# A relational graph convolution on one core: below tile 420, half as many tiles fetched by single row copies

## The chip, the cores and the metric

The kernel runs on one core of one Trainium2 chip. The metric is the device time of one execution in microseconds, the median of several runs. A profile comes from one further execution. Its engines are called PE (TensorE), DVE (VectorE), ACT (ScalarE), POOL (GpSimd) and SP (SyncE); "PEld" is PE's loading of weights.

## What is computed

There are 12500 nodes with 256 features each and 212500 edges, sorted by their destination; every node has one edge to itself. Each edge has one of eight types.

```
h   = relu(layernorm(x))                       # 12500 x 256
hx  = einsum('ni,rio->rno', h, weight)         # one product for each of 8 types
msg = hx[edge_type, src]                       # one row for each edge
agg = segment_sum(msg, dst)                    # 12500 x 256
out = x + agg * sqrt(0.5) + bias + (h @ loop_weight) * sqrt(0.5)
```

## The kernel before, in words

The kernel first sums and then multiplies: for each node and type it adds up the rows of h of the edges that end there, and only then multiplies with the type's weights. So the work has two halves.

**Edge tiles.** The edges are cut into tiles of 128. There are 1581 of them, two to a unit, in the order of the destinations. For tile t, the 128 rows of h of its edges' sources are brought from HBM into a buffer `msg[t]` of SBUF, 128 partitions by 256 numbers, 131 KB. DVE makes a one-hot matrix (line 967) that says for each edge to which of some 13 or 17 near destinations and which type it belongs. PE multiplies the two (line 1005, `edge_sums`; four matmuls a tile in the profile), and DVE adds a unit's sums to a ring of accumulators in SBUF (line 1031).

**Groups of nodes.** When the last edge of a group of 128 nodes is in, PE multiplies the group's sums with the weights (line 1187, `product`), DVE adds x (lines 1200, 1201), and SP writes four groups at a time to the output (line 1206).

**How the rows come.** The first 100 tiles or so are gathered from x and normalised in SBUF, while h is being made and written to HBM; all later ones come from h. There are two ways to bring a tile.

- *Gathered*: one instruction on GpSimd's queue (`gather`, line 915), an indirect DMA with 128 row numbers.
- *Fetched row by row*: 128 copies of one row of 1 KB each (`load_sources` and `fetch_row`, line 939). The SP queue issues rows 0 to 31 and 64 to 95, the ACT queue the other 64. The row number is loaded into a register first. The copies count up one of four semaphores, and PE waits for that count before the tile's sums (`edge_sums`).

`single_rows(t)` decides which tiles are fetched: one in 28 (`SINGLE`), t mod 28 = 27, once h has been ready for long enough, and not in the last 16 tiles. The first such tile is 167 and the last 1539; these are 50 tiles, 6400 row copies. The other 1531 tiles are gathered.

**What sets the order.** The program is written out by hand as a loop over t with fixed places for all work; each engine's queue runs in that order. In step t the loop issues gathers up to tile `goal(t)`, which stands 64 tiles ahead of t until t = 170, then less by one every five tiles, down to 24 from t = 370 on. A gather waits for the sums of the unit that was the last in the program when it was issued ("no faster than the sums"). The buffers `msg` hold 66 tiles (33 pairs). A fetched tile is begun (`begin_fetch`) 36 tiles ahead of its sums (`FAR`), or further ahead where the gathers stand further ahead; its loads come 8 steps later (`HOLD`), and then the loop issues up to four row copies on each of the two queues in each step (`FETCH`). A fetch also waits until the sums of the fetched tile four before it are done, as there are four counters.

The same SP queue issues the 512 KB loads of x and h for the groups (line 1137), the writes of the output (line 1206) and the loads of the indices (line 393); ACT's queue issues small loads of indices (line 405). ACT also clears some of the ring at the beginning (line 1040).

Of the kernel before, what the change touches and what calls it, by code (L numbers as in the profile page):

```python
# [62 lines left out]
SINGLE = 28  # L63
# [2 lines left out]
BY_SP = (0, 2)  # L66
HOLD = 8
FAR = 36
COUNTERS = 4


# [173 lines left out]
def kernel(  # L245
# [64 lines left out]
    def place_of(t):  # L310
        u, i = divmod(t, PAIR)
        half = 0 if PAIR * u + 1 == NT else PAIR - 1 - i
        b, row = row_of(u)
        return b, half, row


    with ExitStack() as main:
# [32 lines left out]
        single, fetches = {}, {SP: [], ACT: []}  # L350
        counters = [tc.alloc_semaphore(f"rows{i}") for i in range(COUNTERS)]
        fetched, summed = {}, {}
# [532 lines left out]
        def single_rows(t):  # L885

            return (t % SINGLE == SINGLE - 1 and t + 2 * NEAR < NT
                    and state["h32"] is not None and t // QUAD * QUAD >= state["h32"] + LATE + AHEAD)

        def begin_fetch(t):  # L890

            if t not in msg:
                room(t - t % PAIR)
            fetched[t] = len(fetched)
            for k, r in enumerate(range(0, P, SOURCES)):
                engine = SP if k in BY_SP else ACT
                fetches[engine].append((
                    done["tile"] + HOLD,
                    lambda r=r, engine=engine: load_sources(t, r, engine)))

        def gather(t):
            if t % PAIR == 0 and t not in msg:
                room(t)
            if t % QUAD:
                kind[t] = kind[t - 1]
            else:
                kind[t] = "h" if state["h32"] is not None and t >= state["h32"] + LATE else "x"
            table = {"h": h32, "x": x}[kind[t]]
            b, i, u = place_of(t)
            if single_rows(t) and t not in fetched and t - done["tile"] >= FAR:  # L910
                begin_fetch(t)
            if t in fetched:
                return
            at = i * P + u
            i = nc.gpsimd.indirect_dma_start(  # L915
                out=msg[t], out_offset=None, in_=table[:, :],
                in_offset=bass.IndirectOffsetOnAxis(ap=gidx[b][:, at : at + 1], axis=0))
            if "unit" in latest:
                tc.add_manual_dep(
                    i.ins, latest["unit"], SYNC_DEP, reason="no faster than the sums")  # L920

        def goal(t):

            lead = max(NEXT, AHEAD - max(0, t - NARROW) // SLOPE)
            lead = min(lead, max(CLOSE, (NT - t) // SLOPE))
            return min(t + lead + 1, STARTED + STEEP * (t // PAIR * PAIR))

        def load_sources(t, r0, engine):
# [9 lines left out]
            def fetch_row(i, v):  # L938
                j = queue.dma_start(
                    msg[t][r0 + i : r0 + i + 1, :].bitcast(U8), h32_bytes[:, bass.ds(v, D * 4)])  # L940
                j.then_inc(counters[k % COUNTERS], 16)
                tc.no_tile_sem_insts.add(j.ins.name)
                tc.add_to_no_dep_group(f"rows{t}", j.ins)
                if i == 0 and k >= COUNTERS:
                    tc.add_manual_dep(
                        j.ins, summed[k - COUNTERS], SYNC_DEP, reason="counter is at rest")

# [37 lines left out]
        def edge_sums(t):  # L985
# [14 lines left out]
            if t in fetched:  # L1000
                k = fetched[t]
                j = nc.tensor.wait_ge(counters[k % COUNTERS], 16 * P * (k // COUNTERS + 1))
                tc.declare_fence(j.ins, group=f"rows{t}")
# [229 lines left out]
        with tc.manual_schedule():  # L1233
# [129 lines left out]
            for t in range(NT):  # L1363
                done["tile"] = t
                if t + FAR >= gathered and single_rows(t + FAR):
                    begin_fetch(t + FAR)
                while gathered < min(NT, goal(t)):
# [125 lines left out]
```

## Time and profile before

| | |
|---|---|
| time, median of 3 runs (lowest to highest) | 1981.88 us (1979.95 to 1982.96) |
| the profiled execution's own time | 1982.09 us |
| span of its profile, first to last instruction | 1980.4 us |
| mean granted clock of PE | 0.949 |
| row copies on the SP queue, on the ACT queue | 3200, 3200 |
| gathers from h, from x | 1431, 100 |
| DMA over the span | 279.45 MB, mean 141 GB/s |

Busy time in the page is the time in which an engine worked on something; "idle before" stands with the group in front of which the engine had nothing to do, and the name behind the arrow is what ended that. A DMA that GpSimd issues counts as busy time of GpSimd for as long as it is being issued, not until the data is there. Issues on the SP and ACT queues aren't counted as busy at all; they are seen in the timeline and in the view of a line.

### The profile page before, as it was taken

What the parts mean: (1) busy time and instruction counts of PE and PEld (TensorE: products, weight loads), DVE (VectorE), ACT (ScalarE), POOL (GpSimd) and SP (SyncE); (2) the same over time, 40 slices, a digit from 0 to 9 for tenths busy, and PEclk for the clock granted to TensorE, in tenths of its full rate; (3) what the DMA queues carried; (4) which work ended last, traced back from release to release, by engine and by line L of the source; (5) the groups of instructions that cost most, each with busy time, mean ns of one, the idle gap of its engine ahead of it and who ended that gap; (6) DMA issues with size and microseconds to landing.
All of it is one profiled execution on the core that took longest, in us unless ns stands there. A gap on an engine that the chain in (4) does not pass through costs nothing. (4 is left out here: it accounts for less than half of the span.)

```text
span 1980.4 us, 41340 instructions
## 1 busy us (share of the span) xinstructions
PE 1711.7 (86%) x10161; PEld 1473.8 (74%) x10161; DVE 1309.2 (66%) x3272; ACT 159.2 (8%) x334; POOL 1457.9 (74%) x1557
## 2 busy tenths in 40 slices
PE   2348999998899888889998898888989989899998
PEld 1247898997777777778777777777777767687897
DVE  6769767886665677656678565578666567665653
ACT  6777200000000000000000000000000000000000
POOL 7677776677777777777777777777777777777774
PEclk8559999999999999999999999999999999999999
DMA  7993444443444444444434444444444344444432
GB/s 252 358 301 103 126 126 134 140 140 107 138 128 122 149 132 120 141 130 121 149 111 141 132 119 143 141 119 141 129 122 142 109 144 130 120 140 125 127 115 78
DMA packets 158363, 279.45 MB, mean 141 GB/s; under 512 B 35376, under 2 KB 109126, under 8 KB 158118
## 3 DMA queue, kind: packets, MB, share of 16 engines
q0 software_dynamic: 73488, 200.77, 34.5%
q1 hardware_dynamic: 76584, 72.73, 11.9%
q10 hardware_dynamic: 8046, 3.30, 0.9%
q8 instruction: 80, 1.31, 0.3%
q14 instruction: 165, 1.35, 0.2%
HBM read 251.06 MB, written 25.60 MB: 140 GB/s over the span
## 5 line engine op out<-in xcount | busy, mean ns | idle before, releaser
L915 POOL DMA_INDIRECT msg<-h,gidx x1431 | 1361.2, 951 | 458.6 <-issue 335.6
L1005 PEld LDWEIGHTS ps<-oh,msg 128*128 128x128 f32 x6324 | 942.1, 198 | 408.1 <-DMA msg<-h,gidx 258.7
L1005 PE MATMUL ps<-oh,msg 128*128 128x136 f32 (+2 forms) x6324 | 1022.8, 291 | 226.3 <-DMA msg<-h,gidx 139.0
L1187 PE MATMUL po<-w,acc 128*128 128x256 f32 x3136 | 891.0, 389 | 15.4 <-DVE acc L1031 15.3
L1031 DVE TENSOR_TENSOR acc<-acc,ps 128x352 f32 x791 | 408.8, 517 | 413.0 <-PE ps L1005 402.1
L1187 PEld LDWEIGHTS po<-w,acc 128*128 128x128 f32 x3136 | 519.0, 193 | 52.1 <-DVE acc L1031 18.6
L1069 DVE SCALAR_TENSOR_TENSOR acc<-types,pt 128x256 f32<-128x256 bf16 (+1 forms) x688 | 247.3, 411 | 67.6 <-PE pt L1051 61.9
L967 DVE TENSOR_TENSOR oh<-fixed,cols 128x544 f32<-128x544 f32 (+1 forms) x396 | 285.8, 722 | 0.0
L915 POOL DMA_INDIRECT msg<-in_x_dram,gidx x100 | 94.8, 948 | 41.4 <-issue 30.1
L1187 PE MATMUL po<-wl,self_t 128*128 128x256 f32 x392 | 115.5, 420 | 3.5 <-DVE acc L1031 1.8
L1187 PEld LDWEIGHTS po<-wl,self_t 128*128 128x128 f32 x392 | 73.8, 210 | 12.6 <-DVE acc L1031 3.1
L853 ACT ACTIVATE msg<-msg,shift,rstd 128x256 f32<-128x256 f32 x100 | 50.8, 586 | 4.4 <-DVE stats L817 3.6
L853 ACT ACTIVATE xt<-xt,shift,rstd 128x256 f32<-128x256 f32 x98 | 50.0, 587 | 7.0 <-DVE shift L850 6.1
L809 DVE BATCH_NORM_STATS2 stats<-xt 128x6 f32<-128x256 f32 x98 | 34.3, 412 | 23.5 <-DMA xt<-in_x_dram 22.7
L1200 DVE TENSOR_TENSOR xr<-xr,po 128x256 f32<-128x256 f32 x98 | 40.4, 412 | 13.4 <-PE po L1187 12.2
L1123 DVE CAST types<-pt 128x512 bf16<-128x512 f32 x22 | 15.2, 691 | 49.6 <-PE pt L1119 49.6
L1056 DVE COPY self_t<-pt 128x256 f32<-128x256 f32 x98 | 40.7, 415 | 8.5 <-PE pt L1051 5.4
L1051 PE MATMUL pt<-ident,hr 128*128 128x128 f32 x196 | 38.9, 281 | 7.2 <-DMA hr<-h 5.3
L442 DVE TENSOR_SCALAR moves<-fixed 128x271 int32<-128x271 int32 (+1 forms) x90 | 40.6, 452 | 4.4 <-DVE acc L1031 3.0
L1201 DVE TENSOR_TENSOR xr<-xr,po 128x256 f32<-128x256 f32 x98 | 41.2, 421 | 3.4
L444 DVE COPY_PREDICATED fixed<-moves,fixed 128x311 int32<-128x311 int32 (+14 forms) x90 | 38.0, 422 | 3.1
L1051 PEld LDWEIGHTS pt<-ident,hr 128*128 128x128 f32 x196 | 25.6, 153 | 10.6 <-DMA hr<-h 5.6
(162 smaller groups left out, 349.1 us busy)
## 6 DMA issues: line engine op xcount, KB each, us to landing
msg<-h ACTq DMA_DIRECT2D x3200, 1.0 KB
msg<-h SPq DMA_DIRECT2D x3200, 1.0 KB
msg<-h,gidx POOLq DMA_INDIRECT x1431
xt<-in_x_dram SPq DMA_DIRECT2D x24, 512.0 KB
h<-xt SPq DMA_DIRECT2D x24, 512.0 KB
xr<-in_x_dram SPq DMA_DIRECT2D x24, 512.0 KB
hr<-h SPq DMA_DIRECT2D x24, 512.0 KB
out_dram<-xr SPq DMA_DIRECT2D x24, 512.0 KB
```

Of the source, the lines that this page charges most:

```text
L442: nc.vector.tensor_single_scalar(m, packed[:, :n], 1 << (bit + k), op=ALU.bitwise_and)
L853: nc.scalar.activation(row, row, AF.Relu, bias=shift[:n, j : j + 1], scale=rstd[:n, j : j + 1])
L915: i = nc.gpsimd.indirect_dma_start(out=msg[t], out_offset=None, in_=table[:, :], in_offset=bass.IndirectOffsetOnAxis(ap=gidx[b][:, at : at ...
L967: j = nc.vector.tensor_tensor(o[:, k : k + v, :i, :width], iota_f[:, :width].unsqueeze(1).unsqueeze(1).to_broadcast([P, v, i, width]), of. ...
L1005: j = nc.tensor.matmul(ps[:, c, first : first + width], m[:, c * P : (c + 1) * P], o[:, :width], start=(i == 0 and c == 0), stop=(end and ...
L1031: i = nc.vector.tensor_tensor(a, a, ps, op=ALU.add)
L1051: in_run("turns", nc.tensor.transpose(pst[:, c, :n], rows_[:n, c * P : (c + 1) * P], ident[:n, :n]), c == KC - 1)
L1056: nc.vector.tensor_copy(got["self", g][:, :, :n], pst[:, :, :n])
L1069: i = nc.vector.scalar_tensor_tensor(acc[:, :, r, s0 : s0 + n], of, float(r + 1), pst[:, :, :n], op0=ALU.is_equal, op1=ALU.mult)
L1187: i = nc.tensor.matmul(got["out", g][:n], lhs, rhs, start=(r == R and c == 0), stop=(r == R - 1 and c == KC - 1))
L1200: nc.vector.tensor_add(rows_[:n, k, :], rows_[:n, k, :], outs[g % 2][:n, 1, :])
L1201: nc.vector.tensor_add(rows_[:n, k, :], rows_[:n, k, :], got["out", g][:n])
```

## The change

`single_rows` gets one more condition. From tile 420 (`SPARSE`) on it decides as before. Below 420 only tiles with t mod 56 = 27 are still fetched row by row; the others are issued by `gather` as any other tile, in their place in GpSimd's queue.

```diff
+SPARSE = 420
@@ def single_rows(t):
             return (t % SINGLE == SINGLE - 1 and t + 2 * NEAR < NT
+                    and (t >= SPARSE or t % (2 * SINGLE) == SINGLE - 1)
                     and state["h32"] is not None and t // QUAD * QUAD >= state["h32"] + LATE + AHEAD)
```

The function is asked in the loop (for tile t + 36) and in `gather`. Nothing else in the text of the kernel changes. The counters of the fetched tiles are given out in turn, so later fetches use other ones of the four than before.

## The prediction

> **What bounds the kernel now.** I read the costliest groups of the page first, then the chain that ended last, then GpSimd's line by stretches of time. The question was which engine's lateness becomes the end.
>
> ```profile
> PE 1711.7 (86%) x10161; PEld 1473.8 (74%) x10161; DVE 1309.2 (66%) x3272; ACT 159.2 (8%) x334; POOL 1457.9 (74%) x1557
> ...
> L915 POOL DMA_INDIRECT msg<-h,gidx x1431 | 1361.2, 951 | 458.6 <-issue 335.6
> L1005 PEld LDWEIGHTS ps<-oh,msg 128*128 128x128 f32 x6324 | 942.1, 198 | 408.1 <-DMA msg<-h,gidx 258.7
> ...
> L915 POOL DMA_INDIRECT msg<-in_x_dram,gidx x100 | 94.8, 948 | 41.4 <-issue 30.1
> ```
>
> GpSimd is 74% busy by the first row, yet its gathers and the idle time in front of them are 1361.2 + 458.6 + 94.8 + 41.4 = 1956.0 us of the 1980.4 us span. PE's weight loads wait 258.7 us for gathers. In a quiet place, GpSimd alone (the timeline: start, duration, instruction, idle time before it):
>
> ```profile
> 700.09 0.95 POOL L915 DMA_INDIRECT msg<-h,gidx  x1 [0.30 <-PE ps L1005]
> ...
> 711.34 0.95 POOL L915 DMA_INDIRECT msg<-h,gidx  x1 [0.30 <-issue]
> ```
>
> Ten gathers, nine steps, 11.25 us: a gather costs **1.25 us** of GpSimd, 0.95 busy and 0.30 that is there before every one of them. The end hangs on the last gather (the chain that ended last, in order of time):
>
> ```profile
> 1953.92 0.95 POOL msg L915
> 1954.86 0.30 issue
> 1955.17 2.79 DMA msg<-h,gidx
> 1957.96 0.04 issue
> 1958.00 0.86 PE ps L1005 x4
> ```
>
> So the last 26 us begin with one of GpSimd's last gathers and its landing, and what follows is PE's. A gather more costs 1.25 us, and a pause of GpSimd beyond 0.30 us costs its length, unless GpSimd is held back anyway.
>
> Where does it pause? First two stretches from the groups view limited to a window (count; busy, mean ns; idle before): 230 to 286 us and 286 to 566 us.
>
> ```profile
> L915 POOL DMA_INDIRECT msg<-h,gidx x45 | 42.6, 948 | 14.1 <-issue 10.4 <-PE ps L1005 2.5 <-DMA msg<-h,gidx 0.9
> ```
>
> ```profile
> L915 POOL DMA_INDIRECT msg<-h,gidx x210 | 199.3, 949 | 80.9 <-issue 44.3 <-DMA msg<-h,gidx 21.1 <-PE ps L1005 14.0
> ```
>
> Then 566 to 902 us, as long as both together, from the view of line 915 (idle time and number of times, by what ended it):
>
> ```profile
> L915 POOL DMA_INDIRECT msg<-h,gidx x267: 940/946/1279, 565.1 to 901.1; - x134
> ...
>   issue: 64.5, 207
>   PE ps L1005: 9.5, 31
>   DMA msg<-h,gidx: 6.7, 22
>   PE po L1187: 1.2, 4
> ```
>
> From 230 to 286 us the idle time is 14.1 / 45 = 0.313 us a gather. From 566 to 902 us it is about 82.8 / 267 = 0.310 (the four rows and 0.9 in smaller ones). From 286 to 566 us it is 80.9 / 210 = 0.385. **The excess is 80.9 - 210 x 0.310 = 15.8 us**; against 0.313 it is 15.2, against the bare 0.30 it is 17.9.
>
> What are the pauses? The same view says below who waited for line 915. The first fence is 230 to 566 us (its first row is still of the list of idle time), the second 566 to 902 us:
>
> ```profile
>   PE ps L1005: 16.5, 39
> ...
>   POOL msg L915: 23.9, 41
> ```
>
> ```profile
>   PEld ps L1005: 62.5, 88
>   PE ps L1005: 33.3, 49
> ```
>
> In the first stretch GpSimd's own gathers waited 41 times for an earlier gather to land; in the second only PE did. The pauses that the view puts down to PE I count with these, since the same gathers wait for both; if they are PE's own, 16.5 - 39 x 0.30 = 4.8 us of the excess would stay. One pause is of another kind: 1.95 us at 293.47, ended by nothing that the profile shows.
>
> ```profile
> 284.90 0.94 POOL L915 DMA_INDIRECT msg<-h,gidx  x1 [0.71 <-PE ps L1005]
> ...
> 288.06 0.94 POOL L915 DMA_INDIRECT msg<-h,gidx  x1 [0.97 <-DMA msg<-h,gidx]
> ...
> 293.47 0.94 POOL L915 DMA_INDIRECT msg<-h,gidx  x1 [1.95 <-issue]
> ...
> 304.57 0.95 POOL L915 DMA_INDIRECT msg<-h,gidx  x1 [1.41 <-DMA msg<-h,gidx]
> ```
>
> Why are landings late just there? The row copies of line 939 are densest there (issues on the ACT and SP queues, first 230 to 566 us, then 566 to 902 us):
>
> ```profile
> L939 ACTq DMA_DIRECT2D msg<-h x767: 217/228/825, 229.7 to 565.8; - x192
> ...
> L939 SPq DMA_DIRECT2D msg<-h x704: 227/228/1229, 232.4 to 558.6; - x176
> ```
>
> ```profile
> L939 ACTq DMA_DIRECT2D msg<-h x641: 227/228/761, 566.1 to 901.8; - x161
> ...
> L939 SPq DMA_DIRECT2D msg<-h x610: 227/228/937, 580.3 to 901.8; - x153
> ```
>
> 1471 rows in 336 us are 4.4 a us; 1251 are 3.7 a us, and there GpSimd doesn't pause. The two queues run one tile's fetch after the other (the timeline of ACT's queue):
>
> ```profile
> 229.68 23.33 ACTq L939 DMA_DIRECT2D msg<-h  x64
> ...
> 255.52 6.39 ACTq L939 DMA_DIRECT2D msg<-h  x19
> ...
> 262.04 96.90 ACTq L939 DMA_DIRECT2D msg<-h  x237
> ```
>
> A fetch of 64 rows takes 23.3 us of a queue. The first pause comes at 284.90, after two fetches on end: one fetch does not do it, a chain of them does.
>
> **The change, part by part.** Fetched row by row are the tiles with t mod 28 = 27 from 167 on; below 420 these are 167, 195, ..., 419, ten. The new condition keeps t mod 56 = 27: 195, 251, 307, 363, 419. **Out go 167, 223, 279, 335 and 391.** From 447 on nothing changes in the rule.
>
> *Added: five gathers on GpSimd.* 5 x 1.25 = **+6.25 us**. They come while GpSimd is the engine that sets the end, so nothing hides them. If each were as long as the longest above, 1279 ns in place of 946, it would be 7.9 us; less than 5 x 0.95 = 4.7 can't be.
>
> *Removed: 5 x 128 row copies, with the register loads in front of them.* On the queues this is 5 x 23.3 us each, off the path: no engine's work waits for a queue in the chain that ended last. Removed on PE: five waits on a counter of rows. PE had no idle time at all at 230 to 286 us (56.00 busy of 56.00, below), so I cost them at nothing; covered they are by PE's own queue of work.
>
> *Moved: the density of the rows.* Without the five, the stretch 230 to 566 us has 1471 - 640 = 831 rows, 2.5 a us, well below the 3.7 at which GpSimd doesn't pause. Nor can the rest bunch up: a fetch's buffer is that of a tile 66 back, so the next kept fetch can't start until PE is there, some 56 tiles after the last one's.
>
> ```profile
> 230.00:286.00 56.00, 56.00 (x375) 51.88 (x372) 33.90 (x70) 3.82 (x2) 42.02 (x45) 1.00 0.49 142
> 286.00:566.00 280.00, 264.11 (x1662) 235.14 (x1661) 201.26 (x482) 0.00 (x0) 199.25 (x210) 0.98 0.45 128
> 566.00:902.00 336.00, 301.22 (x1784) 253.12 (x1784) 217.83 (x517) 0.00 (x0) 253.51 (x267) 0.96 0.45 132
> ```
>
> Columns: PE, weight loads, DVE, ACT, GpSimd busy with counts, granted clock, DMA share, GB/s. Line 1005 has four matmuls a tile, so its count gives PE's pace:
>
> ```profile
> 230.00:566.00 336.00, 192.01 (x1268) 185.72 (x1267) 0.98 0.46 131
> 566.00:902.00 336.00, 178.36 (x1112) 161.05 (x1111) 0.96 0.45 132
> ```
>
> 317 tiles in the first 336 us, 1.06 us a tile: 56 tiles take 59 us, in which a queue fetches for 23.3 us. One fetch and then a rest is what the trace shows before its first pause. **So of the 15.8 us I let 14.0 go**: the odd 1.95 us pause (1.65 over the usual 0.30) stays, and 0.2 us for a chance meeting with a 512 KB load. The ends are 0 and 17.9.
>
> *What is late next.* PE must use the time. It is full at first (56.00 of 56.00), but that is while it has gathered tiles in stock; from 566 to 902 us it waits for gathers:
>
> ```profile
> L1005 PE MATMUL ps<-oh,msg 128*128 128x104 f32 (+1 forms) x1112 | 178.7, 288 | 34.8 <-DMA msg<-h,gidx 33.6
> ```
>
> 33.6 us of idle time in 336 us: PE takes up a lead of 8 us in about 80 us, long before the end. Then GpSimd bounds as before.
>
> **Sum**, against the profiled execution's own 1982.1 us: 1982.1 + 6.25 - 14.0 = 1974.3. The median of the runs shown, 1981.9, is 0.2 below that execution, so I forecast **1974.1 us**.
>
> The rule that bears on the disputed term: the Trainium skill, page "DMA: Bandwidth & Descriptors", section "Why a DMA increments its semaphore by 16 and not by 1", says that a copy issued from SP or ACT runs on k of the 16 engines, the lowest-numbered, with k set by the shape, while a GpSimd transfer counts all 16. By it a copy of one row could lie on few engines, or one, which every gather needs too; then the whole excess goes with the rows, as I have it. No row here names an engine.
>
> **The rivals.**
>
> *Slower: landings are late by the sum of the traffic.* A gathered tile moves the same bytes as a fetched one. If the 16 DMA engines' common load makes landings late, the pauses stay, and the five gathers are added: 1981.9 + 6.25 = 1988.1 us. It decides from the point where the DMA share, not the rows a us, goes with the pauses. For it: the pauses end with landings. Against it: the share is 0.45 with the pauses and 0.45 without (above), and 0.49 at 230 to 286 us without. Chance 0.09. The same page's section "Issuing engines are not separate DMA queues" speaks for this rival: whoever starts a DMA, it runs on the same 16 engines. The equal shares in the trace don't agree that this is all.
>
> *No change: half of the pauses stay.* One fetch of 23 us may be enough when a 512 KB load falls into it, or when the kept fetches from 363 on still meet. Then 7 us go: 1981.9 + 6.25 - 7 = 1981.1 us. For it: pauses are found up to 566 us, where PE is no longer full. Against it: 566 to 902 us has the loads and no pauses. Chance 0.16.
>
> *More than forecast.* The odd pause goes too and GpSimd runs at the bare 0.30: 1981.9 + 6.25 - 17.9 = 1970.2 us; this is the forecast's own lower end.
>
> That the change doesn't do what it says is excluded by the count of tiles above.
>
> **How the numbers follow.** Forecast 0.75 (1970.2 to 1978), half 0.16, slower 0.09. The range is 1970 to 1981: it leaves out the slower rival and the upper half of the second, 0.17. About 0.2%, 4 us, is what a measurement of this kernel can tell from no change: faster than 1977.9 us 0.75, within 0.15, slower than 1985.8 us 0.10.
>
> **What would show it.** GpSimd: 1436 gathers from h in place of 1431. From 286 to 566 us some 221 gathers in place of 210 with idle time near 0.31 us each, and hardly a wait of a gather for a gather. Row copies: 2880 on each queue, about 830 in all from 230 to 566 us. From 566 us on the same 0.31. I am wrong if the pauses are there with 2.5 rows a us (the slower rival), or if GpSimd's pauses go and PE's waits for gathers after 566 us grow instead of the end coming nearer.

## The result, and the profile after

The kernel after takes **1977.7 us** (median of 10 runs, 1974.7 to 1979.8), the kernel before 1983.0 in the same comparison (10 runs, 1980.0 to 1988.2). The ratio is **0.9968, 95% interval 0.9959 to 0.9976**, that is 5.3 us faster. The forecast was 7.8 us faster. In two series of the runs below (e1 to e4 and e7 to e9) the kernel before took 2400 us in place of 1980; the same kernels were run again where it took 1980 (e5 and e10 to e12), and those runs decide.

The profiled execution of the kernel after took 1979.8 us, the longest of the ten. Line numbers are larger by one or two than before: 917 is the gather, 941 the row copy. First the stretch of the pauses, 286 to 566 us, GpSimd's group of gathers (count; busy, mean ns; idle before):

```profile
L917 POOL DMA_INDIRECT msg<-h,gidx x224 | 213.1, 951 | 68.4 <-issue 53.4 <-PE ps L1007 7.3 <-DMA msg<-h,gidx 5.5
```

224 gathers where there were 210, and 68.4 / 224 = 0.305 us of idle time each in place of 0.385. I take 0.305 as the bare rate below; the kernel before has the same from 690 to 810 us, 29.3 / 96 (shown further down), where no gather waits longer. Who waited for line 917 in that stretch (us, times):

```profile
  PEld ps L1007: 8.6, 12
  POOL msg L917: 5.5, 18
  PE ps L1007: 4.8, 7
```

Gathers still wait for gathers 18 times, but 5.5 / 18 = 0.31 us is the usual gap: the pauses are gone. The row copies from 230 to 566 us:

```profile
L941 ACTq DMA_DIRECT2D msg<-h x452: 217/228/907, 251.8 to 566.0; - x151
...
L941 SPq DMA_DIRECT2D msg<-h x384: 227/228/367, 251.9 to 550.1; - x192
```

836 rows, 2.5 a us, as forecast. So far the profile is the one that was forecast. But here is a place that was not, GpSimd from 690 to 810 us, before and after:

```profile
L915 POOL DMA_INDIRECT msg<-h,gidx x96 | 91.3, 952 | 29.3 <-issue 21.4 <-PE ps L1005 4.9 <-DMA msg<-h,gidx 2.4
```

```profile
L917 POOL DMA_INDIRECT msg<-h,gidx x92 | 87.2, 948 | 33.6 <-issue 24.7 <-DMA msg<-h,gidx 4.3 <-PE ps L1007 3.1
```

Four gathers fewer, and 33.6 - 92 x 0.305 = **5.5 us of new pauses**. What is different there? ACT's queue, first before, then after, then SP's queue after:

```profile
608.71 2.45 ACTq L939 DMA_DIRECT2D msg<-h  x7
611.20 4.23 ACTq L405 DMA_DIRECT2D spans<-in_dst_dram  x8
615.52 284.59 ACTq L939 DMA_DIRECT2D msg<-h  x563
```

```profile
480.04 123.66 ACTq L941 DMA_DIRECT2D msg<-h  x246
603.73 45.88 ACTq L406 DMA_DIRECT2D spans<-in_dst_dram  x8
649.70 170.49 ACTq L941 DMA_DIRECT2D msg<-h  x402
```

```profile
642.70 0.41 SPq L1208 DMA_DIRECT2D out_dram<-xr  x1
643.16 0.51 SPq L1139 DMA_DIRECT2D hr<-h  x1
```

The eight small loads of index spans (`load_indices`) took ACT's queue 4.23 us before and take 45.88 us after. Six go out by 606 us. The seventh goes at 646.57, when SP's write of the output, issued at 642.70, has landed, and the eighth at 649.30, when SP's load of h, issued at 643.16, has:

```profile
646.57 3.04 ACTq L406 DMA_DIRECT2D spans<-in_dst_dram  x2
```

In the compiled program these DMAs of SP and ACT share eight completion semaphores in turn (the trace has the number of each), and with the change the two loads get the semaphores of that write and that load of h. Then ACT catches up: 402 rows in 170.5 us, 0.42 us each, where before a row took 284.6 / 563 = 0.51 us. It is a second dense stretch, of 490 rows from 690 to 810 us (4.1 a us) where the kernel before has 460 (3.8). First before, then after:

```profile
L939 SPq DMA_DIRECT2D msg<-h x234: 227/228/937, 690.0 to 809.8; - x117
...
L939 ACTq DMA_DIRECT2D msg<-h x226: 227/228/474, 689.6 to 810.0; - x113
```

```profile
L941 ACTq DMA_DIRECT2D msg<-h x278: 227/228/600, 690.0 to 802.1; - x139
...
L941 SPq DMA_DIRECT2D msg<-h x212: 227/228/1037, 689.9 to 793.2; - x106
```

*What a pause is.* The semaphore events kept in the traces show it one step further. The gathers use eight semaphores in turn, and a landing counts its semaphore up in 16 steps. From the start of a gather to the 15th and to the last step it takes, for the gathers with all 16 steps on record:

| | gathers | 15th step, median | last step, median | last step, longest |
|---|---|---|---|---|
| before, 286 to 566 us | 155 of 210 | 2.8 us | 8.7 us | 12.3 us |
| after, 286 to 566 us | 184 of 224 | 2.7 us | 3.3 us | 7.9 us |
| before, 690 to 810 us | 77 of 96 | 2.8 us | 4.1 us | 7.3 us |
| after, 690 to 810 us | 75 of 92 | 2.8 us | 8.2 us | 10.9 us |

So 15 of the 16 steps come as early with dense row copies as without; one is late. In the kernel before, 286 to 566 us, 26 of the 28 idle times over 0.35 us end 0.76 to 0.79 us after the last step of the gather eight before, which has the same semaphore. They make 14.9 of the pauses' 16.8 us, and 9 of them, 4.2 us, are among those that the views put down to PE. Eight gathers take 8 x 1.25 = 10.0 us, so a pause should begin where the last step comes later than about 10.0 - 0.76 = 9.2 us after the start; the earliest that ended a pause there came after 9.5. In the second dense stretch of the kernel after, 6 of 8 pauses, 2.5 of 5.5 us, end that way; what ends the other two, at 696.67 and 799.15 us, isn't shown.

The accounts from 286 us on, in us against 0.305 a gather: five gathers + 6.25; pauses from 286 to 566 us - (80.9 - 210 x 0.305) = - 16.9; new ones + 5.5. A last pause of the kernel before lay just behind the first stretch, at 575.14 us (566 to 690 us, before and after):

```profile
L915 POOL DMA_INDIRECT msg<-h,gidx x98 | 93.8, 957 | 31.2 <-issue 25.1 <-PE ps L1005 2.7 <-DMA msg<-h,gidx 2.4
```

```profile
L917 POOL DMA_INDIRECT msg<-h,gidx x100 | 94.8, 948 | 30.5 <-issue 23.5 <-PE ps L1007 4.6 <-DMA msg<-h,gidx 1.5
```

31.2 - 98 x 0.305 = 1.3 us of it is gone too. The sum is 6.25 - 16.9 + 5.5 - 1.3 = **- 6.4 us**, inside the interval (4.8 to 8.1 us). The two profiled executions themselves differ by 2.3 us only, as this one lost 4 us before 230 us (167 gathers done where the other had 171), ahead of the first fetch; the later profiles of kernels with the change (e5, e6, e10) had done 169 to 171 there.

### The profile page after: what moved, and what is told of

Its sections match the earlier page's. It is cut to its first block, busy times and chain, and to the rows that moved or that the text cites. A ratio compares the mean times of both kernels' runs of the same rounds, so it can differ in the third digit from the quotient of the medians.

```text
span 1978.1 us, 40031 instructions
## 1 busy us (share of the span) xinstructions
PE 1708.0 (86%) x10161; PEld 1465.9 (74%) x10161; DVE 1308.6 (66%) x3272; ACT 159.3 (8%) x334; POOL 1463.7 (74%) x1562
## 5 line engine op out<-in xcount | busy, mean ns | idle before, releaser
L1189 PE MATMUL po<-w,acc 128*128 128x256 f32 x3136 | 889.0, 388 | 15.3 <-DVE acc L1033 15.3
```

The costliest lines, as they stand in the source:

```text
L1189: i = nc.tensor.matmul(got["out", g][:n], lhs, rhs, start=(r == R and c == 0), stop=(r == R - 1 and c == KC - 1))
```

## The experiments

Theory A: dense row copies make gathers land late, which holds up GpSimd; a gather more costs 1.25 us. Theory A2: the standstill of ACT's queue makes the second dense stretch. Rivals: B, the sum of the traffic makes landings late; C, the added gathers fall into idle time; D, the new pauses are chance.

**The relief without the price.** The kernel after, and in `gather` the five tiles of the change (167, 223, 279, 335 and 391) are not brought at all; the messages of the tile before stand in for theirs:

```diff
+        def dropped(t):
+            return 167 <= t < 420 and t % 56 == 55
...
+            if dropped(t):
+                msg[t] = msg[t - 1]
+                return
```

> The kernel after, but the five tiles 167, 223, 279, 335 and 391 are neither fetched nor gathered: PE multiplies the rows of the tile before them a second time (so these five tiles' own rows are left out). It shows the relief without the price. Theory A (dense row copies make gathers land late; a gather more costs 1.25 us): the kernel after, 1977.7, less 5 x 1.25 = 1971.4 us, ratio to the kernel before 0.994, and no pause of GpSimd from 286 to 566 us (0.31 us of idle time a gather). Rival B (the sum of the traffic makes landings late): only 5 of some 270 tiles' bytes are missing there, the pauses of 15 us stay, about 1982 us. Rival C (the five gathers cost nothing, as they fall into idle time): 1977.7 us.

> The same kernel as e1_neither (the kernel after, the five tiles neither fetched nor gathered; their own rows are left out), where the kernel before takes about 1983 us. Theory A: ratio of the kernel after, 0.9968, less 6.25 of 1983: 0.9936, and no pause from 286 to 566 us. Rival B (the sum of the traffic): about 1. Rival C (the five gathers cost nothing): 0.9968.

> The kernel of e1_neither and e7_neither_again (the kernel after, the five tiles neither fetched nor gathered; their own rows are left out), for a call in which the kernel before takes about 1980 us. Theory A: 0.9968 - 0.0032 = 0.9936, with the standstill of ACT's queue still in it, so that pauses are found from 690 to 810 us and none from 286 to 566 us. Rival B: about 1. Rival C: 0.9968.

Measured: 0.9944 (0.9919 to 0.9969) and 0.9918 (0.9892 to 0.9944) in the series of 2400 us; **0.9926 (0.9912 to 0.9940)** where the kernel before took 1982.9 us: 1968.4 us, 14.6 us faster. GpSimd from 286 to 566 us and from 690 to 810 us in that last run:

```profile
L923 POOL DMA_INDIRECT msg<-h,gidx x223 | 211.8, 950 | 69.1 <-issue 51.4 <-DMA msg<-h,gidx 8.3 <-PE ps L1013 7.0
```

```profile
L923 POOL DMA_INDIRECT msg<-h,gidx x94 | 89.2, 949 | 31.9 <-issue 21.9 <-DMA msg<-h,gidx 4.7 <-PE ps L1013 4.1
```

Idle time 0.310 a gather in the first stretch: the pauses go, but for 1.1 us, with the five fetches, whether their tiles are gathered (the kernel after) or not brought at all. B would have kept them in both, so B falls. Against the kernel after this one is 0.9968 - 0.9926 = 0.0042 of 1983, 8.3 us, faster, give or take 3 us by the two intervals: 6.25 for five gathers, and 2.3 as its second stretch has 31.9 - 94 x 0.305 = 3.2 us of pauses and not 5.5. C, by which only those 2.3 us would be left, falls where the pauses are gone: a gather costs about its 1.25 us there.

**The price without the relief.** The kernel before, which still fetches all ten tiles row by row; the five are gathered besides, into a tile that nobody reads (`dropped` as above):

```diff
-            if t in fetched:
+            if t in fetched and not dropped(t):
                 return
...
-                out=msg[t], out_offset=None, in_=table[:, :],
+                out=unused if dropped(t) else msg[t], out_offset=None, in_=table[:, :],
```

> The kernel before, all ten tiles fetched row by row as there, and for the five tiles a gather of the same rows besides, into a tile that nobody reads any more: the price without the relief. Theory A: 1983.0 + 5 x 1.25 = 1989.2 us, with the pauses from 286 to 566 us as before (about 15.8 us over 0.31 a gather). Rival C (they fall into idle time that is there anyway): 1983 us.

> The same kernel as e2_both (the kernel before, and the five tiles gathered besides into a tile that nobody reads), where the kernel before takes about 1983 us. Theory A: 6.25 us more, ratio 1.0032, the pauses from 286 to 566 us as in the kernel before, 15.8 us over 0.31 a gather. Rival C (the gathers fall into idle time that is there anyway): 1.000.

> The kernel of e2_both and e8_both_again (the kernel before, the five tiles gathered besides into a tile that nobody reads), for a call in which the kernel before takes about 1980 us. Theory A: ratio 1.0032, idle time of GpSimd from 286 to 566 us about 0.385 us a gather as in the kernel before. Rival C: 1.000.

Measured: 1.0078 (1.0047 to 1.0110) and 1.0075 (1.0046 to 1.0105) in the series of 2400 us; **1.0013 (1.0004 to 1.0022)** where the kernel before took 1982.9 us, 2.8 us (0.8 to 4.4) and not the 6.25 of theory A. GpSimd from 286 to 566 us, the useful and the useless gathers:

```profile
L918 POOL DMA_INDIRECT msg<-h,gidx x209 | 198.3, 949 | 78.8 <-issue 45.7 <-DMA msg<-h,gidx 19.5 <-PE ps L1008 8.1
```

```profile
L918 POOL DMA_INDIRECT unused<-h,gidx x4 | 3.8, 951 | 1.2 <-issue 1.2
```

213 gathers, 80.0 us idle: pauses of 80.0 - 213 x 0.305 = 15.0 us in place of 16.9, and the 1.3 us behind 566 us are gone here too. 6.25 - 1.9 - 1.3 = 3.1 us. So C holds in part where the pauses stay: about half of the price is taken out of the pauses. That this is because a gather that waits for an earlier one's landing waits less if GpSimd spent 1.25 us on another in between is likely but not shown.

**Number of copies, or bytes?** The kernel before, with as many row copies, each of half a row (512 B); PE multiplies the first half of such a tile twice:

```diff
-                    msg[t][r0 + i : r0 + i + 1, :].bitcast(U8), h32_bytes[:, bass.ds(v, D * 4)])
+                    msg[t][r0 + i : r0 + i + 1, : D // 2].bitcast(U8), h32_bytes[:, bass.ds(v, D * 2)])
...
-                    ps[:, c, first : first + width], m[:, c * P : (c + 1) * P], o[:, :width],
+                    ps[:, c, first : first + width], m[:, :P] if t in fetched else m[:, c * P : (c + 1) * P], o[:, :width],
```

> The kernel before, with as many row copies, but each of 512 B in place of 1 KB; PE uses the first half of such a tile twice (so the second half of the fetched tiles' rows is left out). It tells the number of copies from their bytes. If the number of copies makes the gathers land late: pauses of about 15 us from 286 to 566 us as before, 1983 us. If the bytes do (B, or bytes on one engine): pauses under 8 us, 1969 to 1976 us.

> The same kernel as e3_half_rows (the kernel before with row copies of 512 B in place of 1 KB; the second half of the fetched tiles' rows is left out), where the kernel before takes about 1983 us. If the number of copies makes gathers land late: 15 us of pauses from 286 to 566 us and a ratio of 1.000. If their bytes do: under 8 us of pauses, ratio 0.993 to 0.997.

> The kernel of e3_half_rows and e9_half_rows_again (the kernel before with as many row copies of 512 B in place of 1 KB; the second half of the fetched tiles' rows is left out), for a call in which the kernel before takes about 1980 us. If the number of copies makes gathers land late: idle time of GpSimd from 286 to 566 us about 0.385 us a gather as in the kernel before, ratio 1.000. If their bytes do: under 0.34 us a gather, ratio 0.993 to 0.997.

Measured: 0.9991 (0.9964 to 1.0017) and 0.9995 (0.9978 to 1.0012) in the series of 2400 us; **0.9984 (0.9976 to 0.9993)** where the kernel before took 1980.3 us. From 286 to 566 us:

```profile
L915 POOL DMA_INDIRECT msg<-h,gidx x212 | 200.7, 947 | 80.0 <-issue 50.0 <-DMA msg<-h,gidx 18.0 <-PE ps L1005 8.8
```

0.377 us a gather against 0.385: pauses of 80.0 - 212 x 0.305 = 15.3 us against 16.9. Halving the bytes took a tenth of these pauses, and 3.2 us of the time (1.4 to 4.8), while taking away half of the ten fetches ends the pauses. The ratio lies between the two that were expected, nearer to that of the copies: it is their number, for the most part. The semaphores agree: the last step of a gather still comes 8.1 us after its start (median, at most 12.6; 163 gathers), the 15th after 2.8.

**The standstill of ACT's queue.** The kernel after, with the third block's small loads on SP's queue:

```diff
-            queue = nc.scalar if b > 1 else nc.sync
+            queue = nc.scalar if b > 1 and b != 3 else nc.sync
```

> The kernel after, with the eight small loads of index spans of the third block of edges issued on SP's queue in place of ACT's. In the kernel after, ACT's queue stands still from 606 to 647 us at these loads, and then fetches without a rest until some 800 us, and GpSimd pauses some 5 us more than before between 690 and 805 us. Theory A2 (that standstill makes a second dense stretch): no standstill, no pauses there, 1977.7 - 5 = 1972.7 us, ratio 0.9948. Rival D (those pauses are chance, or come with the earlier end of the first stretch): 1977.7 us, ratio 0.9973.

> The same kernel as e4_spans_sp, once more: in that call the kernel before took 2400 us in place of 1983, and GpSimd's gathers waited for landings throughout, so that it could not tell of the five us between 690 and 805 us. Where the kernel before takes about 1983 us: theory A2 (the standstill of ACT's queue makes a second dense stretch) 1972.7 us, ratio 0.9948, no pauses from 690 to 805 us; rival D 1977.7 us, ratio 0.9973. Where it takes 2400 us again: ratio 1.00 as before.

Measured: 1.0019 (0.9994 to 1.0044) in the series of 2400 us, which can't tell of 5 us; **0.9940 (0.9926 to 0.9953)** where the kernel before took 1979.6 us: 1968.8 us. ACT's queue, and GpSimd from 690 to 810 us:

```profile
479.83 343.14 ACTq L941 DMA_DIRECT2D msg<-h  x681
```

```profile
L917 POOL DMA_INDIRECT msg<-h,gidx x96 | 90.8, 946 | 29.3 <-issue 23.5 <-DMA msg<-h,gidx 3.0 <-PE ps L1007 2.1
```

No standstill, 343.14 / 681 = 0.50 us a row, and 96 gathers with 0.305 us each as in the kernel before. From 0.9968 to 0.9940 is 5.5 us, give or take 3 us by the two intervals: what the new pauses were. The last step of a gather comes after 4.3 us again there (median, at most 7.4; 78 gathers). A2 holds. D falls: e10, where the eight loads take ACT's queue 43.76 us, has such pauses too, 3.2 us, and this run has none.

**Fewer gathers, fetches in pairs.** The same, and in `single_rows`:

```diff
-                    and (t >= SPARSE or t % (2 * SINGLE) == SINGLE - 1)
+                    and (t >= SPARSE or t not in (223, 307, 391))
```

> As e5_spans_sp_again, but only three of the ten tiles below 420 are gathered, 223, 307 and 391, so that the fetches stand in pairs with a rest behind each (167, 195, then 251, 279, then 335, 363, then 419). Theory A: two fetches on end made no pause in the kernel before, so the relief is nearly whole and the price is 3 x 1.25 in place of 5 x 1.25: 1972.7 - 2.5 = 1970.2 us, ratio 0.9935, at most 3 us of pauses from 286 to 566 us. If pairs are too dense: pauses of 5 to 8 us there, 1975 to 1978 us.

Measured: **0.9942 (0.9929 to 0.9956)**, 1969.5 us: as good as with five (1968.8 us in the same series), not 2.5 us better. From 286 to 566 us:

```profile
L917 POOL DMA_INDIRECT msg<-h,gidx x222 | 210.7, 949 | 70.3 <-issue 52.9 <-PE ps L1007 7.0 <-DMA msg<-h,gidx 6.7
```

70.3 - 222 x 0.305 = 2.6 us of pauses are back; they eat the two gathers saved. All of the long ones lie before 294.1 us, at the first pair of fetches (tiles 167 and 195), which the kernel before has too; behind the later pairs there are none. So two fetches on end are about the point where pauses begin. This version and the one with five are the fastest of those that bring every tile, some 11 us faster than the kernel before.

## Why the prediction was right, and where it was not

*What bounds the kernel.* Right. Every time above where the kernel before took 1980 us follows from GpSimd's gathers and pauses alone, within about 1 us.

*The price, + 6.25 us, "nothing hides them".* Right as the change makes it: 8.3 us, give or take 3, between the kernel after and the one with neither, 2.3 of them the second stretch. As a rule it was too strict: with the pauses left in place the same gathers cost 2.8 us.

*The relief, 14.0 us of 15.8.* Right in kind, too small: 16.9 + 1.3 = 18.2 us went. Of the 4.2 us between, 1.1 is the rate that I count from, 0.305 and not 0.310 a gather. I had kept 1.8 us, most of it for the pause of 1.95 us at 293.47, which nothing explained; it is gone too, and so are the 1.3 us behind 566 us, which I didn't count. In pairs (e6) such a pause comes back, 2.04 us at 294.01, so it belongs to the dense stretch in some way; how is open, as no landing of the gather eight before ends it. The doubt whether the pauses that the view puts down to PE would stay is settled: they end with landings, as shown above.

*"From 447 on nothing changes in the rule", "From 566 us on the same 0.31".* **This step failed.** The rule for those tiles is unchanged, but ACT's queue is one queue for fetches and index loads, and with the change two of its loads came to wait for DMAs of SP that were issued only 36 us after the load before them. The sum had no term for it. It cost 5.5 us of the 18.2.

*The sum.* Forecast 6.25 - 14.0 = - 7.75 us; found 6.25 - 18.2 + 5.5 = - 6.4 by the trace, - 5.3 by the medians. That the two are near is luck in part: 4.2 us more relief and 5.5 us of a second stretch, neither foreseen, nearly cancel. The 1977.7 us lie at the upper end of the forecast's 1970.2 to 1978.

*The rivals.* "Slower by the sum of the traffic" is refuted by the profile after and by e10: the DMA share from 286 to 566 us is 0.45 in the kernel before, with the pauses, and 0.45 in the kernel after, without them; and only one of a gather's 16 steps is late. "Half of the pauses stay" was wrong about the place: none stayed, but a third as much arose elsewhere. The rule that I cited from the Trainium skill, "DMA: Bandwidth & Descriptors", section "Why a DMA increments its semaphore by 16 and not by 1", would let a row copy lie on one engine that every gather needs. The traces agree: a row copy is one packet (ACT's queue moved 3200 packets of 1024 bytes for its 3200 row copies before, 2880 for 2880 after), and of a gather's 16 steps one alone is late. No row names the engine.

## What to carry to other kernels

When small copies are put on two queues to relieve a gathering engine, look at how many of them there are a microsecond, not at their bytes: here 4.4 a us over 336 us and 4.1 over 120 us held up the gathers, 3.7 and 3.8 over as long did not. Fetches that stand in a chain cost more than the same ones with a rest between them, so thin them where the consumer is fastest and the queues run without a gap. And after such an edit look through every later stretch of the trace for a queue that stands still: here an issue that waited for another queue's landing moved with the compiled order, and what it held back came out afterwards in a dense burst.

## What the runs showed of the hardware that I had not expected

A gather lands in 16 steps, and dense row copies delay one of them alone: 15 come within 2.8 us (median) in every stretch measured, the last after 3.3 to 8.7 us. GpSimd doesn't feel this until a last step comes more than about 9.2 us after its gather's start, as eight semaphores go round; then it stands still.

So the border is narrow: from 566 to 902 us, at 3.7 row copies a us, the kernel before pauses once, at 575.14 us just behind the dense stretch, while from 230 to 566 us, at 4.4, it loses 17 us. The mean rate isn't all of it, as e6 has 3.0 a us from 286 to 566 us and pauses at its first pair, where from 230 to 286 us it is 4.6; how long the rows come without a rest counts too.
